# A transformer block on one core: self-attention's values projected for two head pairs at once, in PE tiles of 64 rows by 32 columns

## The chip, the cores and the metric

The kernel runs on one core of one Trainium2 chip. A core has a matrix engine (TensorE, "PE" in the profile, with its weight loads listed as "PEld"), a vector engine (DVE), a scalar engine (ACT), a general engine (POOL) and a queue engine (SP), which here issues nearly all DMAs. Each engine works through its own list of instructions in the order of the program, and semaphores tie the lists together. The metric is the device time in microseconds (us) of one execution; less is better.

## The reference

One block on x of shape 2 x 1024 x 256 (two batches of 1024 tokens), everything in float32, with 16 heads of 64:

```python
h = layernorm(x, ln1);  x = attention(h, h,    sa_wq, sa_wk, sa_wv, sa_wo, sa_bo) + x
h = layernorm(x, ln2);  x = attention(h, cond, ca_wq, ca_wk, ca_wv, ca_wo, ca_bo) + x
h = layernorm(x, ln3);  p = h @ ff_w1 + ff_b1
a, gate = p[..., :1024], p[..., 1024:]
out = a * gelu(gate) @ ff_w2 + ff_b2 + x

def attention(xq, xkv, wq, wk, wv, wo, bo):     # 16 heads of 64, so wq is 256 x 1024
    q, k, v = xq @ wq, xkv @ wk, xkv @ wv       # split into heads
    return softmax(q k^T / 8) v @ wo + bo
```

The change concerns one product of the first attention, `v = h @ sa_wv`: 1024 tokens by 256 inputs by 1024 outputs, for each batch.

## The kernel before

**Units and slots.** Self-attention is cut into 16 units (`units`), one for each batch and pair of heads; a pair is 128 columns of q, k and v. A unit has 8 slots, so a loop of 128 slots (`for p in range(SA)`, L1281) covers self-attention; in what follows n = p % 8 is the slot in its unit, and ui the unit. A slot treats 128 queries of both heads of the pair: `scores` (PE tile `s`, L498), the maxima (DVE, L684), the exponents (ACT, L509), and later the division (POOL, L622) and a 32 x 32 block transpose (DVE, L647) that makes `pT`. The keys are split over two groups of partitions, so each slot swaps its maxima and sums between neighbouring blocks of 32 partitions: `exchange(st)`, four small DMAs issued by SP (L519).

**What reads the exchange.** In slot p, `join(p - 1)` computes from the exchanged numbers a difference on POOL (`dd`, L527 and L528), its exponent on ACT (`ee`, L533) and a denominator on POOL (`den`). ACT therefore has, in this order: in slot p the copies of what the projections of slot p - 1 left in PSUM (`flush(stores)`), the exponents of slot p, and then `ee` of slot p - 1.

**The weighted sum.** `self_values` (PE tile `po`, L550) multiplies `pT` by the values, in four slots out of eight: at n = 7 and n = 0 of the next unit for a unit's first 512 queries, at n = 3 and n = 4 of the next unit for the rest. The values `V` of a unit are held twice (index e of `v[r, t, e, ...]`): as projected, and with the upper and lower 64 partitions swapped. Two DMAs make the second copy (`other_half`, L414 and L415).

**Projections.** The other four slots, n = 1, 2, 5 and 6 (and slots 0 to 6 of the first unit), run one item of the list `work`: q, k and then v of the next unit (`self_pieces`), and at n = 6 two pieces of the output projection `py` (L472) of an earlier unit. Layer norm's transposes `ph` (L284) for the next batch or attention come behind the item of n = 5 where there are any. q and k use PE tiles of 64 rows by 32 columns (`project_both`, L367), eight at a time. v uses tiles of 64 rows by 128 columns with 128 moving columns (`project_self_values`, L398), two at a time. For the first unit, v comes in two halves, in slots 1 and 2.

**PSUM.** Two banks (`mm_tile`) take q, k, v and `py` in turn; two (`sum_tile`) take `po`, and four (`ps_s`) the scores. A bank is written anew when its last reader is done: `py` at n = 6 needs the two banks that the item of n = 5 left, which ACT's copies empty in slot 6.

**Weights.** `load_ahead` (L717) issues the loads of unit ui + 2: q at n = 2, k at n = 3, v at n = 7 (three slots later for q and k in the first unit). They stand on SP behind the four exchange DMAs of their slot, and ahead of that slot's projection in the program. Their SBUF tiles come from the pool `w`: two buffers in turn for `wq`, one for `wk` and one for `wv`. When a tile takes over a buffer, the DMA that fills it waits on SP until the last instruction that uses the tile before it is done, wherever that instruction stands in the program. SP keeps to the order of the program.

Cross-attention and the feed-forward part follow with their own loops and reuse the buffers.

Of the kernel before, what the change touches and what calls it, by code (L numbers as in the profile page):

```python
# [13 lines left out]
P = 128  # L14
# [4 lines left out]
def tile_transformer_block(ctx: ExitStack, tc: tile.TileContext, a: dict, out: bass.AP):  # L19
# [106 lines left out]
    def load_slice(name, c0, n, p):  # L126

        own = w[name][:, c0:c0 + n]
        if p != HR:
            return load_rows(wpool, name[3:], f"{name}_{c0}", own, p)  # L130
        t = wpool.tile(
            [P, NH, n], F32, tag=name[3:], name=f"{name}_{c0}", bufs=2 if name[3:] == "wq" else 1)
        for r0 in range(0, P, HR):
            nc.sync.dma_start(out=t[r0:r0 + HR], in_=own.rearrange("(c p) f -> p c f", p=HR))
        return t
# [74 lines left out]


    ends = const.tile([P, DA // 2], F32, tag="ends", name="ends")

    hT, vs, qk, oT = {}, {}, {}, {}

# [173 lines left out]
            else:  # L389
                nc.scalar.copy(dk, own)  # L390

    def project_self_values(v, pv, wt, h, i0, n, soon):

        for i in range(i0, i0 + n):
            for c in range(NH):
                for r in range(2):
                    own = slice(r * HR, (r + 1) * HR)
                    nc.tensor.matmul(  # L398
                        pv[r][:, i * P:(i + 1) * P], lhsT=h[own, c, i * P:(i + 1) * P],
                        rhs=wt[own, c, :], start=(c == 0), stop=(c == NH - 1),  # L400
                        tile_position=(r * HR, 0),
                    )

        def store():
            tiles = [slice(r * GT + i0, r * GT + i0 + n) for r in range(2)]
            for r in range(2):
                nc.scalar.copy(  # L407
                    v[:, tiles[r], 0, :],
                    pv[r][:, i0 * P:(i0 + n) * P].rearrange("p (t d) -> p t d", d=P))
            if i0 + n == GT:  # L410
                move()

        def other_half():
            nc.sync.dma_start(out=v[:QG, :, 1, :], in_=v[QG:, :, 0, :])  # L414
            nc.sync.dma_start(out=v[QG:, :, 1, :], in_=v[:QG, :, 0, :])  # L415

        def move():
            if soon:
                other_half()
            else:  # L420
                later.append(other_half)

        return store

    def costing(n, fn):

# [3 lines left out]
    def self_unit(b, pr):  # L430

        qk["sa", b, pr] = (
            p2.tile([P, S], F32, tag="QT", name=f"q_sa{b}_{pr}"),
            p2.tile([P, S], F32, tag="KT", name=f"k_sa{b}_{pr}"),
            pt_.tile([P, NT, 2, P], F32, tag="V", name=f"v_sa{b}_{pr}"),
        )

    def self_queries(b, pr, m=KB, t0=0):
# [4 lines left out]
    def self_pieces(b, pr):  # L443


        def q():
            self_unit(b, pr)
            return self_queries(b, pr)

        def k():  # L450
            pk = two_banks(f"pk_sa{b}_{pr}")
            project_both(pk, wsl["sa", pr, "k"], hT["sa", b], KB)
            return lambda: take_both(qk["sa", b, pr][1], pk)

        return [costing(2, q), costing(2, k)] + value_pieces(b, pr, 1)

    def value_pieces(b, pr, parts, soon=True):
        n = GT // parts
        return [
            costing(2, lambda i=i: project_self_values(  # L460
                qk["sa", b, pr][2], two_banks(f"pv_sa{b}_{pr}_{i}"), wsl["sa", pr, "v"],
                hT["sa", b], i * n, n, soon))
            for i in range(parts)
        ]

    def out_piece(kind, b, g, t):

# [75 lines left out]
    def weigh(po, v, pT, t):  # L543

        for e in range(2):
            for a2 in range(2):
                r = slice(a2 * QG, (a2 + 1) * QG)
                n = 2 * t + (e ^ a2)
                for d in range(0, 2 * DH, KB):
                    nc.tensor.matmul(  # L550
                        po[a2][d:d + KB, :QH // 2],
                        lhsT=v[r, t, e, d:d + KB], rhs=pT[r, d // DH * NK + n, :],
                        start=(t == 0 and e == 0), stop=(t == NT - 1 and e == 1),
                        tile_position=(a2 * QG, d),
                    )
# [141 lines left out]
    def self_beside(ui):  # L697

        nxt = self_pieces(*units[ui + 1]) if ui + 1 < NU else cross_pieces(*units[0])
        if ui + 1 < NU:  # L700
            work.extend(nxt)
        else:

            work.extend(nxt[:1])
            held.extend(nxt[1:])
        if ui >= HP:
            ob, og = divmod((ui - HP) // HP, NQ)
            t0 = (ui % HP) * 2
            out_pieces("sa", ob, og, out_order("sa")[t0:t0 + 2])
        if ui == 1:  # L710
            norm_beside("sa", 1)
        if ui in (4, 6):
            add_biases("sa", (ui - 4) // 2)
        if ui == NPAIR + 1:
            norm_beside("ca", 0)

    def load_ahead(p):  # L717

        ui, n = divmod(p, 2 * SH)
        for what in "qkv":  # L720
# [61 lines left out]
    def context_values(b, pr):  # L782

        i = (b * NPAIR + pr) // 2
        if i < 2:
            v = vs["own", i] = pt_.tile([P, NM + 2, VC], F32, tag="V", name=f"v_ca{i}")
# [26 lines left out]

        return store
# [221 lines left out]
    def gate_first(n):  # L1039

        pair, f = divmod(n, NF)
        if f == 0:
            one_u = pt_.tile([P, NF, BT], F32, tag="oT" if pair % 2 else "V", name=f"u{pair}_0")
            if pair == 0:
                other = kT.rearrange("p a b -> p (a b)")[:, :NF * BT].rearrange(
                    "p (f t) -> p f t", f=NF)
            else:
                other = pt_.tile([P, NF, BT], F32, tag="oT" if pair % 2 else "V", name=f"u{pair}_1")
# [172 lines left out]
    with tc.manual_schedule():  # L1221
# [57 lines left out]
        work.extend(value_pieces(*units[0], 2, False))  # L1279

        for p in range(SA):  # L1281
            if p % (2 * SH) == 0:
# [209 lines left out]
```

## Time and profile before

| | |
|---|---|
| time, median of 3 runs | 1076.43 us (1075.42 to 1077.2) |
| span of the profiled execution | 1075.6 us |
| TensorE clock granted | 1.000 of full speed |
| PE busy | 1062.3 us (99%), 19300 matmuls |
| DVE, POOL, ACT busy | 882.6, 774.7, 645.4 us |
| value projections, L398 | 1024 matmuls, 61.7 us busy |
| self-attention loop | from 17.5 us to about 700 us |

For the profiled execution only its span is known, 0.8 us below the median of the runs; what lies around the span is not listed. A float32 matmul shows as two records, so counts of matmuls in the profile are twice those of the code. A row of a timeline gives the start and the length of a run of like instructions on one engine. Since a matmul's end is modelled and eight tiles run side by side, the time of a PE stage is best read from its start to the start of the next stage. SP's DMA rows show the time in which SP issued them, and not the transfer.

### The profile page before, as it was taken

The numbers are of one execution on the slowest core, as the hardware profiler recorded it, in microseconds if no ns is written. First come the engines' busy times: TensorE is split into PE (matmuls) and PEld (weight loads), VectorE is DVE, ScalarE is ACT, GpSimd is POOL, SyncE is SP. The second block draws the span as 40 slices with busy tenths as digits, with TensorE's granted clock in tenths as the row PEclk, the third lists the DMA queues.
The fourth block names the chain that finished last, engine by engine and source line by source line (L and its number), as shares of the span: only waits on it lengthen the run. The fifth ranks groups of instructions, "written<-read, shape, count | busy, mean of one in ns | idle before, by whom it ended". The sixth has DMA issues, their size and how long they took to land.

```text
span 1075.6 us, 46812 instructions
## 1 busy us (share of the span) xinstructions
PE 1062.3 (99%) x19300; PEld 701.7 (65%) x19300; DVE 882.6 (82%) x1321; ACT 645.4 (60%) x2068; POOL 774.7 (72%) x1652
## 2 busy tenths in 40 slices
PE   8999999999999999999999999999999999999998
PEld 6556556566565565676655655566766677788998
DVE  5799999998989989999989898968877887655554
ACT  5766766677666666666777676665565564342231
POOL 2677777777777777777777777776666876499884
PEclk9999999999999999999999999999999999999999
DMA  3222122112111121111111101025776545000000
GB/s 91 65 74 48 44 48 53 43 43 50 31 43 31 33 51 34 38 43 24 44 24 34 43 24 38 16 57 138 173 171 169 124 107 113 17 5 16 21 10 30
DMA packets 104726, 60.84 MB, mean 57 GB/s; under 512 B 32378, under 2 KB 95298, under 8 KB 104514
## 3 DMA queue, kind: packets, MB, share of 16 engines
q1 hardware_dynamic: 103138, 57.07, 22.3%
q8 instruction: 152, 2.49, 1.0%
q10 hardware_dynamic: 1376, 0.79, 0.2%
q14 instruction: 60, 0.49, 0.2%
HBM read 27.91 MB, written 2.10 MB: 28 GB/s over the span
## 4 chain that ended last, share of the span: by engine, by line
PE 87%; DVE 3%; DMA 3%; POOL 3%; SPq 2%; issue 1%; ACT 1%; POOLq 0%; DVEq 0%; ACTq 0%
PE po L550 19%; PE s L498 18%; PE py_sa L472 5%; PE py_ca L472 5%; PE pv_sa L398 5%; PE pk_sa L367 4%; PE pq_sa L367 4%; PE pq_ca L367 4%; PE poc L914 4%; PE pb L1035 4%; PE pq L1174 3%; PE pa L1035 2%; PE sc L834 2%; PE pc L1035 2%; DMA st<-st 2%; SPq L519 2%
## 5 line engine op out<-in xcount | busy, mean ns | idle before, releaser
L622 POOL TENSOR_SCALAR p<-p,rd,ee 128x512 f32<-128x512 f32 x512 | 390.3, 768 | 91.3 <-DVE rd L612 88.2
L509 ACT ACTIVATE p<-s,st 128x512 f32<-128x512 f32 x512 | 345.0, 686 | 173.1 <-DVE st L684 170.4
L684 DVE TENSOR_REDUCE st<-s 128x2 f32<-128x1024 f32 x256 | 308.3, 1205 | 58.9 <-issue 18.2
L647 DVE STREAM_TRANSPOSE pT<-p 128x1024 f32<-128x1024 f32 x256 | 302.7, 1218 | 2.2 <-POOL p L622 2.1
L498 PE MATMUL s<-k_sa,q_sa 64*32 64x512 f32 x4096 | 252.9, 591 | 2.9 <-ACT p L509 2.2
L550 PE MATMUL po<-pT,v_sa 64*32 64x256 f32 x8192 | 237.1, 376 | 0.9 <-DVE pT L647 0.9
L550 PEld LDWEIGHTS po<-pT,v_sa 64*32 64x32 f32 x8192 | 172.6, 106 | 76.5 <-issue 30.6
L498 PEld LDWEIGHTS s<-k_sa,q_sa 64*32 64x32 f32 x4096 | 79.5, 106 | 102.9 <-issue 56.2
L851 ACT ACTIVATE p<-sc,neg 128x154 f32<-128x154 f32 x256 | 96.1, 403 | 79.9 <-DVE rden L859 76.3
L862 POOL TENSOR_SCALAR p<-p,rden 128x154 f32<-128x154 f32 x256 | 96.8, 399 | 52.8 <-DVE rden L859 52.6
L509 ACT ACTIVATION_READ_ACCUMULATOR p<-s,st 128x1 f32 x512 | 103.9, 203 | 0.0
L527 POOL TENSOR_TENSOR dd<-st 128x8 f32<-128x8 f32 x128 | 25.6, 200 | 73.8 <-DMA st<-st 70.8
L398 PEld LDWEIGHTS pv_sa<-sa_wv,hT_ln 64*128 64x128 f32 x1024 | 58.5, 188 | 14.2 <-issue 6.7
L398 PE MATMUL pv_sa<-sa_wv,hT_ln 64*128 64x128 f32 x1024 | 61.7, 275 | 0.0
L367 PE MATMUL pq_ca<-hT_ln,ca_wq 64*64 64x512 f32 (+1 forms) x544 | 59.9, 590 | 0.7 <-DMA ca_wq<-in_L_xattn_ca_wq_dram 0.5
L472 PE MATMUL py_ca<-ca_wo,o_ca 128*128 128x256 f32 x256 | 60.2, 383 | 0.0
L472 PE MATMUL py_sa<-sa_wo,o_sa 128*128 128x256 f32 x256 | 59.7, 385 | 0.3 <-ACT v_sa L407 0.3
L840 DVE TENSOR_REDUCE neg<-sc 128x6 f32<-128x924 f32 (+1 forms) x48 | 47.8, 995 | 14.8 <-PE sc L834 14.8
L472 PEld LDWEIGHTS py_sa<-sa_wo,o_sa 128*128 128x128 f32 x256 | 47.3, 190 | 18.4 <-issue 6.9
L367 PE MATMUL pq_sa<-hT_ln,sa_wq 64*32 64x512 f32 (+1 forms) x976 | 56.9, 586 | 0.0
L367 PE MATMUL pk_sa<-hT_ln,sa_wk 64*32 64x512 f32 x960 | 56.1, 590 | 0.3 <-ACT q_sa L382 0.3
L851 ACT ACTIVATION_READ_ACCUMULATOR p<-sc,neg 128x1 f32 x256 | 56.1, 219 | 0.0
(145 smaller groups left out, 1462.3 us busy)
## 6 DMA issues: line engine op xcount, KB each, us to landing
wf<-pT_ca SPq DMA_DIRECT2D x128, 128.0 KB, 2.4
st<-st SPq DMA_DIRECT2D x512, 1.0 KB, 1.8
v_sa<-v_sa SPq DMA_DIRECT2D x32, 256.0 KB, 4.1
sa_wq<-in_L_xattn_sa_wq_dram SPq DMA_DIRECT2D x32, 128.0 KB, 3.4
sa_wk<-in_L_xattn_sa_wk_dram SPq DMA_DIRECT2D x32, 128.0 KB, 3.3
sa_wv<-in_L_xattn_sa_wv_dram SPq DMA_DIRECT2D x32, 128.0 KB, 3.6
ca_wq<-in_L_xattn_ca_wq_dram SPq DMA_DIRECT2D x32, 128.0 KB, 3.4
wf<-in_L_xattn_ff_w_dram SPq DMA_DIRECT2D x12, 256.0 KB
```

Source lines behind the costliest of these rows:

```text
L367: nc.tensor.matmul(pq[r][f:f + m, at:at + n], lhsT=wt[own, c, f:f + m], rhs=h[own, c, t0:t0 + n], start=(c == 0), stop=(c == NH - 1), tile ...
L398: nc.tensor.matmul(pv[r][:, i * P:(i + 1) * P], lhsT=h[own, c, i * P:(i + 1) * P], rhs=wt[own, c, :], start=(c == 0), stop=(c == NH - 1), ...
L472: nc.tensor.matmul(py[:, e * D:(e + 1) * D], lhsT=o[:, i, (t + e) * P:(t + e + 1) * P], rhs=wo[kind][:, g * HP + i, :], start=(i == 0), st ...
L498: nc.tensor.matmul(sc[a4 * KB:(a4 + 1) * KB, j, :], lhsT=q[r, c:c + KB], rhs=k[r, h * HB:(h + 1) * HB], start=True, stop=True, tile_positi ...
L509: nc.scalar.activation(pr[:, j, :], sc[:, j, :], AF.Exp, bias=st[:, 0, 0, i, j:j + 1], accum_out=st[:, 0, 1, i, j:j + 1],)
L550: nc.tensor.matmul(po[a2][d:d + KB, :QH // 2], lhsT=v[r, t, e, d:d + KB], rhs=pT[r, d // DH * NK + n, :], start=(t == 0 and e == 0), stop= ...
L622: nc.gpsimd.tensor_scalar(pr[:, j, :], pr[:, j, :], own["rd"][:, c:c + 1], own["ee"][:, 0, c:c + 1], op0=ALU.mult, op1=ALU.mult,)
L647: nc.vector.transpose(halves[h][:, :, c:c + KB], slots[p]["p"][i].rearrange("p j (n k) -> p (j n) k", k=KB))
L684: nc.vector.tensor_reduce(st[:, 0, 0, i, :], sc[i], AX.X, ALU.max, negate=True)
L851: nc.scalar.activation(pr_[:, j, i, :T], sc[:, j, i * T:(i + 1) * T], AF.Exp, bias=neg[:, j, i:i + 1], accum_out=den[:, j, i:i + 1],)
L862: nc.gpsimd.tensor_scalar(pr_[:, j, i, :T], pr_[:, j, i, :T], rden[:, j, i:i + 1], 1.0, op0=ALU.mult, op1=ALU.mult,)
L1035: nc.tensor.matmul(into[:, :BT], lhsT=lhs, rhs=wh[pair][i], start=first, stop=True, skip_group_check=True)
```

## The change

Values are projected for two units of one batch at once (256 columns of `sa_wv`). The work is cut by tokens instead: piece i of 2 treats four of the eight token tiles for both units. A piece runs in PE tiles of 64 x 32, with 32 tokens as the stationary operand and 256 moving columns; it has 64 matmuls in the code, as q and k have with 512 columns. The results go to `held_v`, a tile of four parts: three rotate over the units, and the fourth holds the swapped copy for the unit at hand. `move_values` makes that copy at n = 5 of the unit itself, right behind SP's exchange of that slot; it is first read at n = 7.

The order of the items changes with the pairing. An odd unit runs q, k and the first value piece of the next two units (n = 1, 2, 5). An even unit from 2 on runs the second value piece, then q, then k (n = 1, 2, 5). The first unit runs both pieces in slots 1 and 2, where the two halves were. The loads of q and k keep their slots; v is loaded in even units alone, for two units at once. `wq` has one buffer instead of two, and cross-attention's `wq` slices alternate between the buffers of `wq` and `wk`. The buffers of the tag "V", which cross-attention and the feed-forward part reused, are replaced by parts of `held_v`.

```diff
@@ load_slice
-        t = wpool.tile(
-            [P, NH, n], F32, tag=name[3:], name=f"{name}_{c0}", bufs=2 if name[3:] == "wq" else 1)
+        tag = "wk" if name == "ca_wq" and c0 // P % 2 else name[3:]
+        t = wpool.tile([P, NH, n], F32, tag=tag, name=f"{name}_{c0}")
@@ load_weights
-        if kind == "sa" or what == "q":
+        if what != "v":
             wsl[kind, pr, what] = load_slice(f"{kind}_w{what}", pr * P, P, HR)
         elif pr % 2 == 0:
-            wsl[kind, pr, what] = load_slice(f"{kind}_w{what}", pr * P, VC, CC)
+            wsl[kind, pr, what] = load_slice(
+                f"{kind}_w{what}", pr * P, VC, HR if kind == "sa" else CC)
@@
+    held_v = const.tile([P, 4, NT, P], F32, tag="held_v", name="held_v")
@@
-    def project_self_values(v, pv, wt, h, i0, n, soon):
-        for i in range(i0, i0 + n):
+    def project_self_values(b, pr, i):
+        own = [unit_values(b, pr + j) for j in range(2)]
+        pv = two_banks(f"pv_sa{b}_{pr}_{i}")
+        wt, h = wsl["sa", pr, "v"], hT["sa", b]
+        for e in range(2):
             for c in range(NH):
                 for r in range(2):
-                    own = slice(r * HR, (r + 1) * HR)
-                    nc.tensor.matmul(
-                        pv[r][:, i * P:(i + 1) * P], lhsT=h[own, c, i * P:(i + 1) * P],
-                        rhs=wt[own, c, :], start=(c == 0), stop=(c == NH - 1),
-                        tile_position=(r * HR, 0),
-                    )
+                    half = slice(r * HR, (r + 1) * HR)
+                    for f in range(0, P, KB):
+                        t0 = (2 * i + e) * P + f
+                        nc.tensor.matmul(
+                            pv[r][f:f + KB, e * VC:(e + 1) * VC], lhsT=h[half, c, t0:t0 + KB],
+                            rhs=wt[half, c, :], start=(c == 0), stop=(c == NH - 1),
+                            tile_position=(r * HR, f),
+                        )
         def store():
...
+            for j in range(2):
+                for r in range(2):
+                    t0 = r * GT + 2 * i
+                    nc.scalar.copy(
+                        own[j][:, t0:t0 + 2, :],
+                        pv[r].rearrange("p (e j d) -> p j e d", e=2, j=2)[:, j])
+    def unit_values(b, pr):
+        return held_v[:, (b * NPAIR + pr + 2) % 3]
+    def move_values(b, pr):
+        v = unit_values(b, pr)
+        for n in range(2):
+            nc.sync.dma_start(
+                out=held_v[n * QG:(n + 1) * QG, 3], in_=v[(1 - n) * QG:(2 - n) * QG])
@@ self_beside
         if ui + 1 < NU:
+            if ui % 2 == 0 and ui:
+                work.append(value_piece(*units[ui], 1))
             work.extend(nxt)
+            if ui % 2:
+                work.append(value_piece(*units[ui + 1], 0))
@@ load_ahead
+            if what == "v" and ui % 2:
+                continue
@@ the loop over p
             if p in ahead:
                 ahead[p]()
+            if p % (2 * SH) == SH + 1:
+                move_values(*units[p // (2 * SH)])
             load_ahead(p)
...
                 run_work(2 if p < SA - SH else 1, h % 2 or h == 0, sum_tile)
-                if p == LAG:
-                    load_weights("sa", units[1][1], "v")
```

More of the change, by code (lines that the diff above doesn't have):

```diff
@@ L390, in take_both @@
                 nc.scalar.copy(dk, own)
-    def project_self_values(v, pv, wt, h, i0, n, soon):
-        for i in range(i0, i0 + n):
+    def project_self_values(b, pr, i):
[3 more added lines that the diff above has]
+        for e in range(2):
             for c in range(NH):
                 for r in range(2):
-                    own = slice(r * HR, (r + 1) * HR)
-                    nc.tensor.matmul(
-                        pv[r][:, i * P:(i + 1) * P], lhsT=h[own, c, i * P:(i + 1) * P],
-                        rhs=wt[own, c, :], start=(c == 0), stop=(c == NH - 1),
-                        tile_position=(r * HR, 0),
-                    )
-        def store():
[L405 to L421, printed above, removed]
-        return store
@@ L434, in self_unit @@
             p2.tile([P, S], F32, tag="KT", name=f"k_sa{b}_{pr}"),
-            pt_.tile([P, NT, 2, P], F32, tag="V", name=f"v_sa{b}_{pr}"),
+            (unit_values(b, pr), held_v[:, 3]),
         )
@@ L453, in k, with value_piece @@
             return lambda: take_both(qk["sa", b, pr][1], pk)
[L455 to L464, printed above, removed]
+        return [costing(2, q), costing(2, k)]
+    def value_piece(b, pr, i):
+        return costing(2, lambda: project_self_values(b, pr, i))
     def out_piece(kind, b, g, t):
@@ L551, in weigh @@
                         po[a2][d:d + KB, :QH // 2],
-                        lhsT=v[r, t, e, d:d + KB], rhs=pT[r, d // DH * NK + n, :],
+                        lhsT=v[e][r, t, d:d + KB], rhs=pT[r, d // DH * NK + n, :],
                         start=(t == 0 and e == 0), stop=(t == NT - 1 and e == 1),
@@ L788, in context_values @@
         if i < 2:
-            v = vs["own", i] = pt_.tile([P, NM + 2, VC], F32, tag="V", name=f"v_ca{i}")
+            v = vs["own", i] = held_v[:, i].rearrange("p t d -> p (t d)").rearrange(
+                "p (n d) -> p n d", d=VC)
             nc.vector.memset(v[:, NM:, :], 0.0)
@@ L1042, in gate_first @@
         if f == 0:
-            one_u = pt_.tile([P, NF, BT], F32, tag="oT" if pair % 2 else "V", name=f"u{pair}_0")
+            spots = [
+                held_v[:, j:j + 2].rearrange("p n t d -> p (n t d)").rearrange(
+                    "p (f t) -> p f t", f=NF) for j in (2, 0)
+            ]
             if pair == 0:
-                other = kT.rearrange("p a b -> p (a b)")[:, :NF * BT].rearrange(
+                spots[1] = kT.rearrange("p a b -> p (a b)")[:, :NF * BT].rearrange(
                     "p (f t) -> p f t", f=NF)
-            else:
-                other = pt_.tile([P, NF, BT], F32, tag="oT" if pair % 2 else "V", name=f"u{pair}_1")
+            elif pair % 2:
+                spots = [
+                    pt_.tile([P, NF, BT], F32, tag="oT", name=f"u{pair}_{j}") for j in range(2)
+                ]
+            one_u, other = spots
             ub[pair] = (one_u, other)
@@ L1278, in tile_transformer_block @@
         work.append(costing(2, lambda: self_queries(*units[0], P, 2 * P)))
-        work.extend(value_pieces(*units[0], 2, False))
+        work.extend(value_piece(*units[0], i) for i in range(2))
         for p in range(SA):
```

## The prediction

> **What bounds the kernel now.** I read the head of the page first, then the chain that ended last around one unit, then that unit's windows.
>
> ```profile
> span 1075.6 us, 46812 instructions
> ...
> PE 1062.3 (99%) x19300; PEld 701.7 (65%) x19300; DVE 882.6 (82%) x1321; ACT 645.4 (60%) x2068; POOL 774.7 (72%) x1652
> ...
> PE 87%; DVE 3%; DMA 3%; POOL 3%; SPq 2%; issue 1%; ACT 1%; POOLq 0%; DVEq 0%; ACTq 0%
> ```
> ```profile
> 209.62 3.45 PE po L550 x128
> 213.07 1.72 PE s L498 x32
> 214.79 3.77 PE pv_sa L398 x64
> ```
> ```profile
> sum 42.75, PE 42.75 PEld 24.93 DVE 39.59 ACT 30.19 POOL 33.95; mean PE 5.34 PEld 3.12 DVE 4.95 ACT 3.77 POOL 4.24
> ```
>
> PE is busy for 99% of the span, and the chain goes from one PE stage to the next without a gap. The third fence sums the eight slots of unit 4 (187.05 to 229.80): PE is busy for all 42.75 us, DVE for 39.59. So a shorter PE stage is worth its full length as long as DVE keeps up, and any wait of PE, however it comes about, is lost for good.
>
> **What the PE stages cost.** These timelines show PE in unit 4 (n = 2 to 7) and in unit 10, where no transposes follow the values; the last row counts the transposes that do.
>
> ```profile
> 199.09 3.64 PE L367 MATMUL pk_sa<-hT_ln,sa_wk 64*32 64x512 f32 x64
> 202.52 1.92 PE L498 MATMUL s<-k_sa,q_sa 64*32 64x512 f32 x32
> ...
> 212.86 1.92 PE L498 MATMUL s<-k_sa,q_sa 64*32 64x512 f32 x32
> 214.72 3.84 PE L398 MATMUL pv_sa<-sa_wv,hT_ln 64*128 64x128 f32 x64
> 218.49 0.66 PE L284 MATMUL ph_ln<-ident,hT_ln 128*128 128x128 f32 x4
> 219.08 1.95 PE L498 MATMUL s<-k_sa,q_sa 64*32 64x512 f32 x32
> 220.96 3.72 PE L472 MATMUL py_sa<-sa_wo,o_sa 128*128 128x256 f32 x16
> 224.61 1.95 PE L498 MATMUL s<-k_sa,q_sa 64*32 64x512 f32 x32
> ```
> ```profile
> 470.27 1.99 PE L498 MATMUL s<-k_sa,q_sa 64*32 64x512 f32 x32
> 472.19 3.84 PE L398 MATMUL pv_sa<-sa_wv,hT_ln 64*128 64x128 f32 x64
> 475.97 1.95 PE L498 MATMUL s<-k_sa,q_sa 64*32 64x512 f32 x32
> ```
> ```profile
> L284 PE MATMUL ph_ln<-ident,hT_ln 128*128 128x128 f32 x32 | 5.3, 287 | 0.0
> ```
>
> From start to start, scores and values together take 475.97 - 470.27 = 5.70 us in unit 10. The new value stage has the shape of `po`, 128 matmul records of 256 columns in 64 x 32 tiles, which takes 3.45 us; scores ahead of such a stage take 1.72. Together 5.17: a gain of 0.5. With transposes behind it, scores, values and transposes take 219.08 - 212.86 = 6.22 us; the new stage has to make the change of tile shape that scores make ahead of `py` (220.96 - 219.08 = 1.88 against 1.72, so 0.16): 1.72 + 3.45 + 0.16 + 0.59 = 5.92, a gain of 0.3. The 32 transposes are eight stages of four, so of the 14 value stages in units 1 to 14, eight gain 0.3 and six 0.5: 5.4 us.
>
> Two rules of the Trainium skill bear on this. TensorEngine Tiling (Array Packing), Key Properties, says that a change of tiling mode drains the engine, so the new shape spares drains; the rows agree and price one at about 0.16 us, within the gain above. The same page, Instruction Overhead, speaks against the change: each matmul has about 60 cycles of overhead, and the new stage has 64 records more. At that price (25 ns at the 2.4 GHz that the skill's TensorE: Matmul & The Clock Gate states in its head table; an estimate) a stage would be 1.6 us longer and the whole change 26 us dearer. The trace disagrees: `po` packs 128 records into the time of `pk_sa`'s 64.
>
> **The first unit.**
>
> ```profile
> 21.99 1.96 PE L498 MATMUL s<-k_sa,q_sa 64*32 64x512 f32 x32
> 23.88 2.06 PE L398 MATMUL pv_sa<-sa_wv,hT_ln 64*128 64x128 f32 x32
> 25.87 1.34 PE L754 MATMUL pk<-ctxT,ca_wk 96*128 96x320 f32 x4
> ...
> 42.96 2.13 PE L498 MATMUL s<-k_sa,q_sa 64*32 64x512 f32 x32
> 45.02 3.84 PE L398 MATMUL pv_sa<-sa_wv,hT_ln 64*128 64x128 f32 x64
> 48.79 1.95 PE L498 MATMUL s<-k_sa,q_sa 64*32 64x512 f32 x32
> ...
> 53.11 1.09 PE L498 MATMUL s<-k_sa,q_sa 64*32 64x512 f32 x16
> ```
>
> Slots 1 and 2 get a whole stage where a half was: scores and half take 25.87 - 21.99 = 3.88, and become 1.72 + 3.45 + 0.16 = 5.33, twice 1.45 more. Slot 5 loses unit 1's values and should fall from 5.83 (42.96 to 48.79) to about slot 6's 4.32 (48.79 to 53.11): -1.5. Net +1.4, so PE as a whole gains 5.4 - 1.4 = 4.0 us. Bounds: 0 (no stage gets shorter but those two) and 5.4.
>
> **The moved projection and the load ahead of it.** The rows are SP's in unit 4, then POOL and ACT in its slots 5 and 6, then SP's exchange rows with their landings.
>
> ```profile
> 205.16 1.82 SPq L134 DMA_DIRECT2D sa_wq<-in_L_xattn_sa_wq_dram  x2
> ...
> 210.71 1.34 SPq L134 DMA_DIRECT2D sa_wk<-in_L_xattn_sa_wk_dram  x2
> 213.03 2.89 SPq L519 DMA_DIRECT2D st<-st  x4
> ...
> 218.20 3.35 SPq L519 DMA_DIRECT2D st<-st  x4
> ...
> 222.28 0.65 SPq L414 DMA_DIRECT2D v_sa<-v_sa  x1
> ```
> ```profile
> 217.14 0.20 POOL L527 TENSOR_TENSOR dd<-st 128x8 f32<-128x8 f32 x1
> 217.43 0.25 POOL L528 TENSOR_SCALAR dd<-dd 128x8 f32<-128x8 f32 x1
> ...
> 218.01 0.22 ACT L533 ACTIVATE ee<-dd 128x8 f32<-128x8 f32 x1
> 218.59 1.07 ACT L407 COPY v_sa<-pv_sa 128x512 f32<-128x512 f32 x2 [0.36 <-PE pv_sa L398]
> ```
> ```profile
> L519 SPq DMA_DIRECT2D st<-st x512: 507/589/1715, 22.8 to 703.0; - x171
> L519 SPq EVENT_SEMAPHORE  x251: 17/28/8183, 12.9 to 701.1; - x126
> ...
> DMA to landing us min/median/max: 1.7/1.8/3.9
> ```
>
> In even units k of the next unit moves from n = 2 to n = 5, but the load of k for the unit after stays at n = 3, and `wk` has one buffer. The load then waits on SP for a projection two slots later. SP keeps its order (its longest wait for a semaphore is 8.183 us), and behind the load stand the exchanges of slots 4 and 5. Perfetto Trace Analysis in the Trainium skill, DMA Instruction — HWDGE, says likewise that the issuing sequencer sits out a DMA's semaphore wait before descriptors are made.
>
> In unit 4's times: scores of slot 5 start at 212.86, k follows at 214.58 and takes 3.43 (199.09 to 202.52), with its last results 0.21 later, at 218.2. SP, which reached the load at 210.71, issues it then (1.34, to 219.6). Four exchange DMAs follow at 0.6 each (the median is 0.589); the fourth starts at 221.4 and lands 1.8 later, at 223.2. Before, `dd` read that exchange at 217.14. Now `dd` takes until 223.7 (0.54 as from 217.14 to 217.68) and `ee` until 224.0. Behind `ee` stand ACT's copies of k; the first frees a PSUM bank at about 224.6 (half of 1.07, and an allowance of 0.1 for the signal). `py` needs that bank. Without the wait it would start at 214.58 + 3.43 + 0.16 + 0.59 + 1.88 = 220.64: PE stands still for 4.0 us, or 4.7 where no transposes (0.75 with their change of shape) fill in. DVE and POOL wait with it, and nothing catches up. It strikes where an even unit from 2 on still loads k: units 2, 4, 6, 8, 10, 12; with transposes behind n = 5 in 4, 6 and 12 (units 3 to 6 and 11 to 14 have them). 3 x 4.0 + 3 x 4.7 = 26.1 us. Bounds for one stall: 3.9 (with transposes, landing in 1.7) and 6.8 (without, landing in 3.9), so 23 to 41.
>
> The load of q waits in even units too, for the projection at n = 2; SP reaches it at 205.16, 2.6 us after that stage ends at 202.52: nothing. Its cover is SP's lag behind PE. v's load at n = 7 waits for n = 1: nothing.
>
> **The swapped copy.** It moves from one unit ahead to n = 5 of its own unit, behind the exchange (218.20 to 221.55) and, in units 1 to 4, one more weight load. `v_sa` was issued at 222.28 before, in n = 6, so SP's time for it hardly changes, but its reader is now `po` at n = 7.
>
> ```profile
> v_sa<-v_sa SPq DMA_DIRECT2D x32, 256.0 KB, 4.1
> ```
>
> The second DMA of the copy is issued at about 222.2 and lands 4.1 later, at 226.3. `po` starts 1.72 after 224.61, less the gain of 0.3, at 226.0, and reads the copy an eighth of its stage (0.4) later: 0.1 to spare, or 0.5 us late with the extra load. I take +1.5 over all units; bounds 0 (both sides of the copy are contiguous now) and 15 x 0.7 = 10.
>
> **What is costed at nothing.** Two ACT copies more for each value stage: ACT has 42.75 - 30.19 us free in a unit. The doubled first load of `sa_wv` has until 23.88. Without that cover each would cost its own length, under a microsecond a unit. The three rotating parts are rewritten one slot after their last reader; cross-attention's v and the gated products take parts that are free by then.
>
> **The sum**, against 1075.6 us of span with 0.8 around it to the median of 1076.4: -4.0 + 26.1 + 1.5 = +23.6, so 1100.0 us.
>
> **The rivals.** (1) The load's wait costs PE nothing: *faster*, 1076.4 - 4.0 = 1072.4. It decides at one point: SP free by 214.2 instead of 218.2, 4.0 us earlier, and `py` never waits. For it: PE idles little today although POOL's `dd` waits for exchanges often. Against it: the order of ACT's rows and the single `wk` buffer. (2) The swapped copy is late in every unit on top, its upper bound: 1100.0 + 8.5 = 1108.5. Against it: the 0.1 us to spare. (3) A stage's time goes by its number of matmuls: 3.43/64 x 128 = 6.86, so 16 x 3.4 = 54 us more, 1154. Against it: `po`'s row. The overhead rule of the Trainium skill named above points this way. (4) Most of the stall is absorbed, a sixth of my price is left and meets the gain: 1076. Against it: PE's 42.75 of 42.75 us.
>
> **How the numbers follow.** Forecast 0.80; (1) 0.10; (2) 0.06; (3) 0.01; (4) 0.03. From the bounds: a low of 1076.4 - 5.4 + 23 = 1094, and a high of 1108.5 with rival (2) at the likely stall; I reach to 1090 for a shorter chain behind the load and to 1110, which leaves out (1), (3), (4) and the longest landings. This kernel's measurement can tell 0.2% (2.2 us) from no change: faster 0.10, same 0.02, slower 0.88.
>
> **What would show it.** The timeline of an even unit should show SP's `sa_wk` issue only after `pk_sa` of n = 5, then `dd` some 6 us late and PE idle ahead of `py` with ACT's copy of k as the releaser, six times; odd units near 42.4 us, and the new stage at 3.45. If `sa_wk` is issued before `pk_sa`, or `dd` comes late and PE does not stop, the forecast is wrong; a gap ahead of `po` at n = 7 speaks for (2).

## The result

The changed kernel takes 1121.83 us, the median of 5 runs (1119.57 to 1124.93), against 1076.43 (1075.42 to 1079.66): the ratio is 1.042, with a 95% interval of 1.04 to 1.0439. The forecast was 1100.0, from 1090 to 1110: the direction was right, but the loss is almost twice as large as forecast, 45.4 us against 23.6.

### The profile page after: what moved, and what is told of

It is laid out like the page before. It is cut to its first block, busy times and chain, and to the rows that moved or that the text cites. A ratio compares the mean times of both kernels' runs of the same rounds, so it can differ in the third digit from the quotient of the medians.

```text
span 1123.1 us, 48877 instructions
## 1 busy us (share of the span) xinstructions
PE 1076.2 (96%) x20324; PEld 718.8 (64%) x20324; DVE 884.0 (79%) x1321; ACT 646.5 (58%) x2098; POOL 776.7 (69%) x1652
## 4 chain that ended last, share of the span: by engine, by line
PE 74%; POOL 7%; DMA 6%; SPq 5%; DVE 3%; issue 2%; ACT 1%; POOLq 0%; ACTq 0%; DVEq 0%
PE po L550 15%; PE s L498 14%; PE py_sa L472 6%; DMA st<-st 5%; SPq L519 5%; PE py_ca L472 4%; PE pq_sa L369 4%; PE pk_sa L369 4%; PE pv_sa L405 4%; PE pb L1042 3%; PE pq L1187 3%; PE pq_ca L369 3%; PE poc L921 3%; POOL p L622 3%; PE pa L1042 2%
## 5 line engine op out<-in xcount | busy, mean ns | idle before, releaser
L684 DVE TENSOR_REDUCE st<-s 128x2 f32<-128x1024 f32 x256 | 308.5, 1206 | 71.4 <-PE s L498 30.5
L498 PE MATMUL s<-k_sa,q_sa 64*32 64x512 f32 x4096 | 259.7, 594 | 5.1 <-ACT p L509 4.5
L550 PE MATMUL po<-pT,held_v 64*32 64x256 f32 x8192 | 241.4, 376 | 1.5 <-DVE pT L647 1.0
L550 PEld LDWEIGHTS po<-pT,held_v 64*32 64x32 f32 x8192 | 179.8, 106 | 71.3 <-issue 27.8
L498 PEld LDWEIGHTS s<-k_sa,q_sa 64*32 64x32 f32 x4096 | 89.0, 107 | 97.6 <-issue 49.0
L472 PE MATMUL py_sa<-sa_wo,o_sa 128*128 128x256 f32 x256 | 74.3, 453 | 28.9 <-ACT k_sa L392 28.4
L472 PEld LDWEIGHTS py_sa<-sa_wo,o_sa 128*128 128x128 f32 x256 | 57.6, 231 | 51.6 <-ACT k_sa L392 33.9
L533 ACT ACTIVATE ee<-dd 128x8 f32<-128x8 f32 x128 | 27.4, 214 | 68.1 <-POOL dd L528 67.5
L405 PE MATMUL pv_sa<-sa_wv,hT_ln 64*32 64x256 f32 x2048 | 60.1, 376 | 0.0
L405 PEld LDWEIGHTS pv_sa<-sa_wv,hT_ln 64*32 64x32 f32 x2048 | 45.2, 106 | 17.5 <-issue 6.5
```

Of the source, the lines that this page charges most:

```text
L405: nc.tensor.matmul(pv[r][f:f + KB, e * VC:(e + 1) * VC], lhsT=h[half, c, t0:t0 + KB], rhs=wt[half, c, :], start=(c == 0), stop=(c == NH - ...
L472: nc.tensor.matmul(py[:, e * D:(e + 1) * D], lhsT=o[:, i, (t + e) * P:(t + e + 1) * P], rhs=wo[kind][:, g * HP + i, :], start=(i == 0), st ...
L498: nc.tensor.matmul(sc[a4 * KB:(a4 + 1) * KB, j, :], lhsT=q[r, c:c + KB], rhs=k[r, h * HB:(h + 1) * HB], start=True, stop=True, tile_positi ...
L550: nc.tensor.matmul(po[a2][d:d + KB, :QH // 2], lhsT=v[e][r, t, d:d + KB], rhs=pT[r, d // DH * NK + n, :], start=(t == 0 and e == 0), stop= ...
L684: nc.vector.tensor_reduce(st[:, 0, 0, i, :], sc[i], AX.X, ALU.max, negate=True)
```

## The profile after

From the head of the changed kernel's page: the span, the busy time of the engines, the row of the granted TensorE clock over 40 slices, and the shares of the chain that ended last. The profiled execution is the longest of the five runs (1124.93 us); the mean granted clock of the five lies between 0.978, in this one, and 0.985.

```profile
span 1123.1 us, 48877 instructions
...
PE 1076.2 (96%) x20324; PEld 718.8 (64%) x20324; DVE 884.0 (79%) x1321; ACT 646.5 (58%) x2098; POOL 776.7 (69%) x1652
...
PEclk9999989989989999998998999999999999999999
...
PE 74%; POOL 7%; DMA 6%; SPq 5%; DVE 3%; issue 2%; ACT 1%; POOLq 0%; ACTq 0%; DVEq 0%
```

PE's share of the chain fell from 87% to 74%, and POOL, the exchange's DMAs and SP came onto it: that is the wait that was forecast. Two things in these lines were not. PE has *more* busy time than before (1076.2 against 1062.3), although its new stages are shorter. And the clock row, which before was an unbroken row of nines (mean 1.000), dips in six slices (mean 0.978). The same work may have taken longer there, and the rows below show that it did.

The groups by line, with idle time and its releaser at the end, name both. The first row is of the kernel before, the others are of the changed kernel:

```profile
L472 PE MATMUL py_sa<-sa_wo,o_sa 128*128 128x256 f32 x256 | 59.7, 385 | 0.3 <-ACT v_sa L407 0.3
...
L472 PE MATMUL py_sa<-sa_wo,o_sa 128*128 128x256 f32 x256 | 74.3, 453 | 28.9 <-ACT k_sa L392 28.4
L405 PE MATMUL pv_sa<-sa_wv,hT_ln 64*32 64x256 f32 x2048 | 60.1, 376 | 0.0
L527 POOL TENSOR_TENSOR dd<-st 128x8 f32<-128x8 f32 x128 | 26.0, 203 | 106.5 <-DMA st<-st 103.2
```

PE stands still for 28.4 us ahead of `py` until ACT has copied k out of PSUM, six times (4.1 to 5.8 us each). And `py` itself, which was not touched by the change and has the same 256 records, takes 74.3 us of PE, where it took 59.7 before. That is 14.6 us on top.

Unit 4 shows one stop from beginning to end. The timelines are SP's, then PE's, POOL's and ACT's; a row has start, length, engine and what runs.

```profile
218.62 3.15 SPq L519 DMA_DIRECT2D st<-st  x4
229.11 1.34 SPq L134 DMA_DIRECT2D sa_wk<-in_L_xattn_sa_wk_dram  x2
230.61 2.47 SPq L519 DMA_DIRECT2D st<-st  x4
...
225.09 3.91 PE L369 MATMUL pk_sa<-hT_ln,sa_wk 64*32 64x512 f32 x64
228.93 0.66 PE L286 MATMUL ph_ln<-ident,hT_ln 128*128 128x128 f32 x4
229.51 1.95 PE L498 MATMUL s<-k_sa,q_sa 64*32 64x512 f32 x32
235.60 6.54 PE L472 MATMUL py_sa<-sa_wo,o_sa 128*128 128x256 f32 x16 [4.14 <-ACT k_sa L392]
...
234.30 0.20 POOL L527 TENSOR_TENSOR dd<-st 128x8 f32<-128x8 f32 x1 [6.48 <-DMA st<-st]
...
234.87 0.21 ACT L533 ACTIVATE ee<-dd 128x8 f32<-128x8 f32 x1 [5.97 <-POOL dd L528]
234.98 1.05 ACT L392 COPY k_sa<-pk_sa 128x512 f32<-128x512 f32 x2
```

SP issues nothing from 221.8 to 229.1. It holds the load of k until `pk_sa` of n = 5 has read the old k (225.09 to 229.0), then sends the exchange that `dd` has been waiting for since 227.8; `ee` follows, then ACT's copies, and PE starts `py` 4.14 us late. Then `py` takes 6.5 us, where its rows before had 3.7.

The windows of the same kernel say why. A row gives a stretch, the busy time (and instructions) of PE, PEld, DVE, ACT and POOL in it, then the granted clock, the DMA share and GB/s. The first two rows are in the first unit, the others in unit 2.

```profile
46.80:50.20 3.40, 1.33 (x30) 0.26 (x8) 2.36 (x4) 1.86 (x5) 1.93 (x5) 1.00 0.04 4
50.20:53.60 3.40, 3.00 (x32) 0.62 (x32) 3.22 (x4) 1.79 (x7) 2.89 (x7) 0.50 0.01 3
138.90:142.30 3.40, 0.00 (x0) 0.00 (x0) 0.17 (x1) 0.00 (x0) 0.20 (x1) 1.00 0.24 56
142.40:145.80 3.40, 2.42 (x6) 1.97 (x7) 1.96 (x3) 3.16 (x9) 3.15 (x8) 0.50 0.20 55
145.80:149.20 3.40, 3.40 (x10) 2.68 (x9) 2.28 (x5) 1.72 (x7) 3.23 (x8) 0.50 0.56 156
149.20:152.60 3.40, 3.40 (x76) 1.74 (x82) 1.47 (x3) 0.59 (x2) 0.47 (x2) 1.00 0.03 5
```

In the 3.4 us of the third row PE does nothing; for the 6.8 us after it the granted clock is exactly half. The trace has one such stretch at each of the six stops, 6.8 us long every time; it begins 1.0 to 2.6 us before `py` does. PE works for 29.8 of these 41 us (for 5.8 in the two rows of unit 2), and half of that, 14.9, is about what `py` lost. A shorter stretch (3.4 us, from 50.20) lies in the first unit, behind a slot in which PE has no item of work, and another from 797.7.

The even units with a stop last 49.2 to 50.0 us, against 42.2 to 43.3 before: +40.8 us over the six (read from the starts of the units' first scores). The other units from 1 to 14 make +0.8 together, and the first unit +2.6 (44.0 against 41.4).

## The experiments

All times are held against runs of the kernel before on the same chip. The theory: what costs is PE's six stops, by the load of k that waits on SP, *and the halved clock that follows each*. The rivals: the new value stage or the new order of the items is itself dearer; the swapped copy is late; or the stops cost only their own length and something else makes up the rest.

**Taking the block away.** Two kernels move one issue and nothing else: the load of k in even units goes from n = 3 to n = 6, behind the projection that it waits for, or to n = 4, one slot later than in the changed kernel.

```diff
@@ load_ahead, changed kernel: k_load_late (k_load_one_slot has at = 4)
+            if what == "k" and ui and ui % 2 == 0:
+                at = 6
```

> The changed kernel with one edit: in even units from 2 on, the load of k is issued at n = 6, behind the projection whose buffer it takes, and no longer at n = 3. Theory A (SP sits on that load, the exchange of slot 4 is late, PE stops ahead of the output projection, and the stop itself makes the granted clock fall to half for 6.8 us): no stop, clock 1.0 in all these units, even units near 42.4 us instead of 49.7, so 1121.8 - 6 x 7.3 = 1078, or a little less. Theory B (the swapped copy or the new value stage is what costs): the late load changes little, over 1110. The price of the pairing without the block is then read against the kernel before: I expect 1072 to 1078.

> As the run above, but the load of k moves by one slot only, from n = 3 to n = 4, so that it still waits on SP for the projection at n = 5, yet stands behind the exchange of slot 4. Theory A, which says that it is this exchange that PE waits for: SP still stands still for some microseconds, but only the exchange of slot 5 is late, by 1 to 2 us, which PE's own work covers; 1073 to 1080, no fall of the clock. If any wait of SP at this place stops PE: over 1095.

With n = 6 the time is 1079.66 us, ratio 1.0033 [1.0018, 1.0048]: moving two DMAs on a queue takes back 41.7 of the 45.2 us (1.042 less 1.0033, of 1076.4), and 1079.66 lies a little above the 1072 to 1078 that were expected. SP's timeline in unit 4, and the group of `py`:

```profile
220.54 2.83 SPq L519 DMA_DIRECT2D st<-st  x4
...
226.46 2.44 SPq L519 DMA_DIRECT2D st<-st  x4
229.00 1.38 SPq L134 DMA_DIRECT2D sa_wk<-in_L_xattn_sa_wk_dram  x2
```
```profile
L472 PE MATMUL py_sa<-sa_wo,o_sa 128*128 128x256 f32 x256 | 59.7, 385 | 0.2 <-ACT k_sa L392 0.2
```

Nothing waits behind the load, the wait ahead of `py` falls from 28.9 to 0.2 us, and `py` is back at 59.7. Units 1 to 14 are together 4.7 us shorter than before: in this execution the new stage and the new order are a small gain in the loop. The rival that they are dearer is out.

With n = 4 the time is 1083.74, ratio 1.0076 [1.0049, 1.0103]. One slot is enough to remove most of the block, but the 1073 to 1080 that were expected are missed: the wait of SP is not all covered. What remains sits in another place. The waits of PE, with total, count and longest:

```profile
PE po L550 <- DMA held_v<-held_v: 3.3, 6, 1.3
```

SP still holds that load for a while (2.4 us, in unit 4), and the swapped copy behind it lands late for `po`: five of the six waits are in units 2, 4 and 10 and make 2.8 us. That is the prediction's rival (2), in three of the six units. The granted clock was 1.0 in the profiled execution, and 0.995 to 0.998 in three of the other five runs.

**The block alone, in the kernel before.** The mirror image: no part of the change but a load issued too early. The load of v for the unit after next goes from n = 7 to n = 3 in units 2, 4, ..., 12; there it waits for v's projection at n = 5, as k's does in the changed kernel.

```diff
@@ load_ahead, kernel before: v_load_early
+            if what == "v" and ui in (2, 4, 6, 8, 10, 12):
+                at = 3
```

> The kernel before with one edit: the load of v is issued at n = 3 instead of n = 7 in units 2, 4, 6, 8, 10 and 12. Its single buffer is in use until the values of n = 5, so SP sits on this load as it does on that of k in the changed kernel; the values keep their old form, and no copy moves. Theory A: the same stop and the same half clock, six times about 7 us, so 1076 + 42 = 1118 (1110 to 1124). Theory B (the stop belongs to the new values or their copy): within 1 us of 1076.

1114.0 us, ratio 1.0355 [1.034, 1.037], so +38.2 us. SP's timeline in unit 4, and the group of `py`:

```profile
216.65 1.34 SPq L134 DMA_DIRECT2D sa_wk<-in_L_xattn_sa_wk_dram  x2
223.84 1.59 SPq L134 DMA_DIRECT2D sa_wv<-in_L_xattn_sa_wv_dram  x2
225.59 2.47 SPq L519 DMA_DIRECT2D st<-st  x4
```
```profile
L472 PE MATMUL py_sa<-sa_wo,o_sa 128*128 128x256 f32 x256 | 70.6, 437 | 27.6 <-ACT v_sa L407 27.6
```

Six stops of 27.6 us in all, and `py` 10.9 us longer (70.6 - 59.7): 38.5, which is the whole difference. One early load makes the loss with the old tiles and the old order of items. Here the clock was half for 3.4 us behind four of the stops and for 6.8 behind two.

**The stop without the halved clock.** To price the two parts separately, PE is kept busy during the stop: nine matmuls of 128 x 128 by 256 columns, whose result nothing uses, behind the scores of n = 6. The block on SP stays. A second kernel has five, which fill some 2 us only.

```diff
@@ the loop over p, changed kernel: filler_full (filler_half has range(5))
             load_ahead(p)
+            if p % (2 * SH) == 6 and p // (2 * SH) in (2, 4, 6, 8, 10, 12):
+                fill = sum_tile(f"fill_{p}")
+                for _ in range(9):
+                    nc.tensor.matmul(
+                        fill[:, :2 * P], lhsT=ident, rhs=kT[:, 0, :2 * P], start=True, stop=True)
```

> The changed kernel with its block left as it is, and with nine matmuls of 128 x 128 x 256 (about 3.9 us) into a spare PSUM bank behind the scores of n = 6 in units 2, 4, 6, 8, 10 and 12, where PE stood still for 4.1 us and more. They compute nothing that is used. Theory A (the stop costs its own length, and then some 2.8 us more because the clock is halved for 6.8 us): the start of the output projection stays where it was, its length falls from 6.5 to 3.65 us, no half clock in these units, so 1121.8 - 6 x 2.8 = 1105. If the halved clock is not a consequence of the stop, or not what costs: 1119 to 1125.

> The new kernel with five matmuls of 128 x 128 by 256 columns, whose result nothing uses, behind the scores of n = 6 in units 2, 4, 6, 8, 10 and 12. They take about 2 us of the 4 to 5.8 us in which TensorE stood still there, so 2 to 3.8 us of stop are left. If a stop must last about as long as the shortest stretch of halved clock (3.4 us) to halve the clock: the stretches of halved clock go in all or nearly all of the six units, py takes 3.65 us again, and the time is 1108 to 1112 us as with nine. If 2 to 2.5 us can be enough (one stop of 2.5 us at 48 us was followed by a stretch of 3.4 us): some of the six keep a stretch of 3.4 us with py some 1.5 longer, and the time is 1112 to 1119 us.

With nine: 1109.68 us, ratio 1.0309 [1.0292, 1.0327]. PE's timeline in unit 4, and the groups:

```profile
230.23 4.15 PE L1318 MATMUL fill<-kT,ident 128*128 128x256 f32 x18
234.46 3.72 PE L472 MATMUL py_sa<-sa_wo,o_sa 128*128 128x256 f32 x16
```
```profile
L472 PE MATMUL py_sa<-sa_wo,o_sa 128*128 128x256 f32 x256 | 59.7, 386 | 5.6 <-ACT k_sa L392 5.5
...
L1318 PE MATMUL fill<-kT,ident 128*128 128x256 f32 x108 | 24.9, 385 | 0.0
```

`py` starts as late as ever, but runs at full clock in all six units. Work that does nothing makes the kernel faster by 11.9 us (1.042 less 1.0309): that is the price of the halved clock, or a little less than its price, since the stops, now 24.9 us of filling and 5.6 of waiting, have grown from 28.4 to 30.5. They are still lost: with the 3.6 of the kernel without a block they make 34.1, against 33.3 measured. The 1105 us that were expected are missed by 4.7: that sum took 16.8 us for the halved clock.

With five: 1110.34 us, ratio 1.0323 [1.0309, 1.0337]. Stops of 1.8 to 2.7 us were left, and three of the six were still followed by a halved clock, for 3.4 us each. The windows, in the columns of above, show one that was and one that wasn't:

```profile
140.10:143.50 3.40, 0.87 (x4) 0.80 (x5) 0.41 (x2) 1.61 (x4) 2.01 (x6) 1.00 0.18 40
143.50:146.90 3.40, 3.40 (x10) 2.69 (x9) 2.50 (x3) 2.36 (x8) 3.14 (x7) 0.50 0.60 165
...
232.20:235.60 3.40, 1.61 (x7) 1.44 (x8) 1.15 (x2) 2.35 (x7) 2.59 (x8) 1.00 0.17 40
235.60:239.00 3.40, 3.40 (x34) 1.89 (x40) 2.49 (x4) 3.01 (x10) 3.31 (x6) 1.00 0.67 193
```

So 2 us of idle time can be enough, which was the second of the two expectations on the clock; the time it forecast for that case, 1112 to 1119, was too high.

**The new tiles without the 256 columns.** The kernel before, with values still projected for one unit at a time and with 128 moving columns, but in tiles of 64 x 32: eight side by side, where tiles of 64 x 128 are two.

```diff
@@ project_self_values, kernel before: narrow_alone
-                    nc.tensor.matmul(
-                        pv[r][:, i * P:(i + 1) * P], lhsT=h[own, c, i * P:(i + 1) * P],
-                        rhs=wt[own, c, :], start=(c == 0), stop=(c == NH - 1),
-                        tile_position=(r * HR, 0),
-                    )
+                    for f in range(0, P, KB):
+                        nc.tensor.matmul(
+                            pv[r][f:f + KB, i * P:(i + 1) * P],
+                            lhsT=h[own, c, i * P + f:i * P + f + KB],
+                            rhs=wt[own, c, :], start=(c == 0), stop=(c == NH - 1),
+                            tile_position=(r * HR, f),
+                        )
```

> The kernel before with one change: values in tiles of 64 x 32 with 32 tokens stationary, still 128 moving columns and one pair of heads at a time; so 256 matmul records of 128 columns in a stage instead of 64 of 128 columns in tiles twice as few at a time. Queue order, loads and the order of the items are those of before. If a stage's time goes by moving columns over the tiles that run side by side: 3.45 us a stage as for po, less than the 3.84 of before, and 1070 to 1074 us in all. If each matmul has a fixed cost of some 25 ns (rival 3 of the prediction in its milder form): 256 x 25 ns = 6.4 us a stage, 2.6 more than before in each of 16 stages, so 1110 to 1125 us. If the time of a record stays at 53 ns as for 512 columns: 13.6 us a stage, over 1200 us.

1106.45 us, ratio 1.0292 [1.0273, 1.0312], so +31.4. The group, and a stage of unit 1 in PE's timeline:

```profile
L399 PE MATMUL pv_sa<-sa_wv,hT_ln 64*32 64x128 f32 x4096 | 68.8, 273 | 24.5 <-issue 24.4
```
```profile
92.28 3.24 PE L399 MATMUL pv_sa<-sa_wv,hT_ln 64*32 64x128 f32 x214
...
96.96 0.85 PE L399 MATMUL pv_sa<-sa_wv,hT_ln 64*32 64x128 f32 x39 [1.44 <-issue]
```

That is between the first two expectations, and nearer to the second. Records start some 15 ns apart (214 in 3.24 us), but PE then pauses for 1.4 us inside the stage with no wait that the profile names ("issue"); over all stages it is 24.4 us, in 20 pauses. Behind three of them the clock was half for 3.4 us. A stage takes 4.8 to 6.5 us, with a median of 5.60 ahead of transposes, 22 ns a record, where 64 records took 3.77. So the number of records is *not* free. The new stage does not pay for it: its 128 records take 3.45 us, 27 ns each, without a pause. Projecting two units at once, which halves the records, is what makes the narrow tiles pay. The last section follows the pauses to the loads of PE's code.

**A version without stops.** The load of k at n = 6, and the first unit's second value piece in two halves, so that its items fill slots 0 to 5 and none is empty.

```diff
@@ changed kernel: late_split (beside the edit of k_load_late)
-    def project_self_values(b, pr, i):
+    def project_self_values(b, pr, i, es=(0, 1)):
...
-        for e in range(2):
+        for e in es:
...
-        work.extend(value_piece(*units[0], i) for i in range(2))
+        work.append(value_piece(*units[0], 0))
+        work.extend(value_piece(*units[0], 1, (e,)) for e in range(2))
```

> The new kernel with the load of k issued at n = 6 in even units, and with the first unit's second value piece cut into two halves (in slots 2 and 3), so that its items of work fill slots 0 to 5 and slot 5 of the first unit has something to do. Theory A (what made the new kernel slow is TensorE standing still, and the halved clock behind each stop): unit 0 falls from 44.5 us in the kernel with the late load alone to 41.5 to 42.5, no granted clock below 1 near 50 us, units 1 to 14 stay some 4.5 us below the kernel before in sum, and the time is 1070 to 1074 us, below the kernel before by 0.2 to 0.6%. Rival (the first unit is longer because the whole stages are dearer than the halves were, wherever the idle slot is): unit 0 stays at 44 or above, and the time stays at 1076 to 1080.

1074.95 us, the median of 11 runs (1072.19 to 1076.5), ratio 0.9992 [0.9983, 1.0001]. From its page:

```profile
span 1071.8 us, 48894 instructions
...
PE 1056.4 (99%) x20324; PEld 695.0 (65%) x20324; DVE 882.8 (82%) x1321; ACT 646.6 (60%) x2102; POOL 778.4 (73%) x1652
```

The first unit falls from 44.5 to 42.0 us as expected, without a halved clock, and PE's busy time is 5.9 us below the kernel before. But the time was forecast at 1070 to 1074 and is 1074.95: against the old kernel's 1075.9 this is no difference that the runs can tell. The profiled execution was among the shortest of this kernel, and its 3.8 us of lead in span is not the typical one.

| from the kernel before | us | from |
|---|---|---|
| the change without a stop or an empty slot (not to be told from 0) | -0.9 | 0.9992 |
| the empty slot in the first unit, with what follows it | +4.4 | 1.0033 less 0.9992 |
| six stops ahead of `py` | +29.7 | 1.0309 less 1.0033 |
| the halved clock behind the stops | +11.9 | 1.042 less 1.0309 |
| the changed kernel | +45.2 | 1.042 |

Of the 4.4 us of the empty slot, the traces show 2.5 in the first unit (44.5 against 42.0). In the profiled execution with the late load, a projection of cross-attention also waited 1.6 us for its weights, and a stretch of halved clock followed; the one with split pieces has no such stretch. Whether that belongs to the empty slot is not shown.

## Why the prediction was wrong

**The mechanism of the block was right, and so, nearly, was its size.** The load of k was issued only after `pk_sa` of n = 5, POOL waited for `dd` (6.5 us in unit 4), and ACT's copy of k released `py`, six times. I priced a stop at 4.0 us with transposes behind n = 5 and at 4.7 without. Measured with transposes (units 4, 6, 12): 4.14, 4.29, 4.26. Without (2, 8, 10): 5.01, 4.97, 5.77. The sum is 28.4 us against 26.1, and the runs give 29.7. The kernel with the early load of v confirms the cause, and moving one issue removes it.

**The step that failed is the price of a stop.** "Any wait of PE, however it comes about, is lost for good" was taken to mean that a wait costs its own length. PE's next stage was priced at the duration that it had in the trace of before, where the clock never left 1.000. Behind a stop it doesn't have that duration: `py` took 5.7 to 6.5 us instead of 3.65 in the six units, 14.6 us by the trace and 11.9 by the kernel with filled stops. The term of 26.1 should have been about 40 (28.4 and 11.9). Its upper bound, 41 us, would have held it, but the bound was there for late landings and I reached only to 1110.

Against the 45.2 us of the table the forecast of 23.6 lacks 21.6. The halved clock is 11.9 of it. The length of the stops adds 3.6 (29.7 against 26.1), the empty slot in the first unit 3.0 (4.4 against 1.4), and the value stage with its copy 3.0 (-0.9 against -5.4 + 1.5).

TensorE: Matmul & The Clock Gate in the Trainium skill, Part 1, states what was needed: the clock is halved after an idle window of about 3.4 us, and the windows run freely. The prediction cited this page for the full clock and left out this rule. As an estimate from that page of the Trainium skill: one window at half clock behind each of six stops of 4 us or more loses half of 3.4 us six times, some 10 us, so 1110. The trace has two windows at each stop, which would be 20 us if PE worked all through them. The runs agree with the rule in kind and differ in the amount of idle time, as the last section shows.

**The first unit** was forecast at +1.4 us and came at +2.6. Slot 5 did fall, to 4.61 us (45.99 to 50.60 in PE's timeline, against 4.32 forecast), but its empty place made PE stand still for 2.47 us, and the slot after ran at half clock:

```profile
45.99 2.13 PE L498 MATMUL s<-k_sa,q_sa 64*32 64x512 f32 x32
50.60 3.40 PE L498 MATMUL s<-k_sa,q_sa 64*32 64x512 f32 x32 [2.47 <-ACT p L509]
53.94 2.42 PE L760 MATMUL pk<-ctxT,ca_wk 96*128 96x320 f32 x8
56.29 1.95 PE L498 MATMUL s<-k_sa,q_sa 64*32 64x512 f32 x32
...
479.69 1.92 PE L498 MATMUL s<-k_sa,q_sa 64*32 64x512 f32 x32
481.41 3.66 PE L405 MATMUL pv_sa<-sa_wv,hT_ln 64*32 64x256 f32 x128
484.86 1.92 PE L498 MATMUL s<-k_sa,q_sa 64*32 64x512 f32 x32
```

The scores at 50.60 take 3.40 us instead of 1.95. It is the same error as with the stops: the slot was priced by the work that is left in it, and neither the stop that takes the place of the work nor the halved clock behind it was in the sum.

**The value stage** was right to the hundredth where it ran undisturbed: scores 1.72 (479.69 to 481.41), values 3.45 (481.41 to 484.86) in eight of ten stages without transposes, and 3.59 in two of four ahead of transposes, against 3.45 + 0.16. The other four took 3.74 to 4.05; why is not shown. Of the 5.4 us that this should bring in units 1 to 14, 4.7 arrive in the kernel with the late load. In the kernel with split pieces 4.0 do, and the runs of the whole kernel show 0.9. How much of it is kept is within what executions of one kernel differ by.

**Rival (3)**, the time by the number of matmuls, was rejected on `po`'s row, and for this change rightly. As a general reading "the trace disagrees" went too far: TensorEngine Tiling (Array Packing) in the Trainium skill, Instruction Overhead, speaks of a fixed price for each matmul, from which the prediction had worked out 25 ns as an estimate. With 128 columns a record takes 22 ns with the pauses and 15 without, where half of a record of the new stage is 13.5: the records do have a price here, and most of it lies in the pauses.

**The swapped copy** was priced at 1.5 us with bounds of 0 and 10. PE's wait for it is 0.5 us in all; the copies land 3.6 us after their issue, against 4.1 before.

**What stays open.** After the loop the profiled execution of the changed kernel loses another 3.3 us against the one of before. 1.7 of it is a stop of PE at 794.4, ahead of a projection of cross-attention that waited for a statistic of layer norm on DVE; 3.4 us of halved clock follow, worth as much again. The kernels with fillers and with the early load of v have no half clock there, and what made DVE late was not looked into.

## What to carry to other kernels

Price a stop of the matrix engine at its own length plus half of what the engine works in the stretch of halved clock that comes with it (here 14.9 us beside 28.4), and look in the row of the granted clock for whether the stages you price from have ever seen a stop. A load that waits for its buffer blocks everything behind it on its queue: when work moves to a later slot, move the loads into its buffers behind it, and when a slot loses its only item, fill it. Narrow tiles multiply the matmuls: here they paid with 256 moving columns (3.45 us a stage against 3.77) and did not with 128 (5.60).

## What was not expected of the hardware

**Half clock after less than 3.4 us of idle time.** Six of the kernels of this case have stretches of exactly half clock before the end of their work, 24 in all in the profiled executions, each 3.4 or 6.8 us long. Within an execution their starts lie on a grid: in the changed kernel 50.2, 142.4, 234.5 and 326.7 are 92.1 to 92.2 us apart, 27 times 3.413. The units repeat at about that distance too, but the last stretch, which is no stop of the loop, fits as well (797.7 is 57 times 3.413 behind 603.2), and so do the two of the kernel with the late load (699.7 us, 205 times). Worked out from the matmul records, PE idled for 1.6 to 3.4 us of the 3.4 ahead of each start. Once the kernels were under way, every such window at full clock with 1.9 us idle or more was followed by a halved one, none under 1.6 was, and between the two both occurred. That the windows run freely agrees with TensorE: Matmul & The Clock Gate in the Trainium skill, Part 1. The limit that it gives under HAM oscillation, no gaps of more than about 3.4 us, is too wide here: the stop of 2.47 us in the first unit halved the clock in the changed kernel, and one of 2.5 us at the same place, 48.2, did not in the kernel with the load at n = 4, whose clock stayed at 1.0 in the profiled execution: there the grid cut the stop, and no window had more than 1.84 us of idle time, against 2.07 in the changed kernel. Where a stop falls on the grid decides. A second halved window followed in all eight cases in which PE idled for 1.0 us or more of the first, and in one of the sixteen in which it idled for 0.4 or less.

**A pause inside a stage of many matmuls.** With 256 records of 128 columns, PE paused for 24.4 us in all without a wait that the profile names; with 128 records of 256 columns the stage has no pause (0.0 us of idle time ahead of L405). The record of the DMA queues points at PE's code. A row has a queue's packets, MB and share; the first is of the kernel with narrow tiles alone, the second of the kernel before:

```profile
q8 instruction: 176, 2.88, 1.1%
...
q8 instruction: 152, 2.49, 1.0%
```

Divided by PE's matmuls and weight loads (twice 22372 and twice 19300), that is about 64 bytes for each in both kernels, in packets of 16 KB: so this queue brings PE's code, some 256 records at a time. A narrow stage has 256 matmuls and 256 weight loads and needs two packets, the new stage one. All 20 pauses end 2.3 to 2.9 us after a packet of this queue started (the one in unit 1 ends at 96.96, behind a packet that started at 94.59); of all records of these stages about one in five starts so. No run was made to test it: that PE waited for its code is argued from these times alone.
